# The weighted selection matrix of layer 1, made on GpSimd in thirds, one pair ahead

## The chip, the core and the metric

The kernel runs on one core of a Trainium2 chip. A core has TensorE (matrix products, PE in the profile), VectorE (DVE), ScalarE (ACT), GpSimd (POOL) and SyncE (SP), which here only issues transfers. Each engine executes its own list of instructions in order, and semaphores make an engine wait for another one or for a transfer. The metric is device time in microseconds.

## The reference, cut to what matters

There are 128 graphs of 64 nodes with 128 features, and one weighted adjacency matrix per graph. About a quarter of its entries are not zero. Four layers follow one another, each with a residual and a layer norm. Layers 0 and 1 compute a filter for every edge and sum messages over a node's edges. Layers 2 and 3 are graph convolutions. Layer 1, which the change is about, is in short:

```python
diff = e[:, :, :, None] - offsets              # 64 gaussians of each edge weight
g = jnp.exp(coeff * diff * diff)
h = ssp(einsum('bijg,fg->bijf', g, W1) + b1)   # ssp is softplus - log 2
Wf = einsum('bijf,gf->bijg', h, W2) + b2       # the filter of edge i, j
rf = einsum('bjd,fd->bjf', r, Wa)
Wf = Wf * Am                                   # Am is the edge weight
y = einsum('bjf,bijf->bif', rf, Wf * Am)       # so each message has the weight squared
y = einsum('bid,ed->bie', ssp(einsum('bif,df->bid', y, Wd1) + bd1), Wd2) + bd2
x = layernorm(x + y)
```

## The kernel before, in words

The first stage packs the edges. Rows are sorted by their number of edges, and each pair of graphs gets lists of "slots", one slot for each edge that is kept, with three values: d (the edge weight), j (the number of the source node, as bf16) and w (the factor of the message; in layer 1 the weight squared). The lists lie in DRAM, written by `pack`.

The main loop takes one pair of graphs after the other, number n from 0 to 127. Pairs 0 to 63 are layer 0, pairs 64 to 127 are layer 1 (`NP` is 64 and `N` is 128). Partitions 0 to 63 belong to the first graph of a pair, 64 to 127 to the second. A pair is worked on in three steps, k = 0, 1, 2, each on a third of its slots; in layer 1 a third has 380 to 420 columns (`CHUNKS`). The loop is a software pipeline over steps i = 3n + k:

- `loads(n + 2)`, at k = 0, issues on SP the transfers of d, j and w for the pair two ahead, in the order d, j, w for each of the two graphs (line 1289). d has three buffers in rotation, j and w two.
- `gaussians(n + 1, k)` makes the gaussians in place in d on ScalarE, for the next pair (a `Square` at k = 0, an `Exp` at k = 1).
- `one_hot(n)`, at k = 0, makes the weighted selection matrix `hot` on VectorE (line 1750). Its row r, column s is w of slot s where j of slot s equals r, and 0 elsewhere. It has two buffers in rotation.
- `filter_in` multiplies the gaussians by W1 (`px`, line 1762), and ScalarE makes the softplus `h`.
- `gather`, for the step before, multiplies the node features by a third of `hot` (`pg`, line 1789): this selects and weighs the source node of each slot. ScalarE copies it to `g`.
- `filter_out` and `message`, for the step before that, multiply `h` by W2 (`pw`, line 1776) and, on VectorE, multiply by `g` (`m`, line 1804). `slot_sums` adds each row's slots (lines 1828 and 1832).

Pairs are joined in groups of four for the work on nodes. `node_after` makes layer 1's output for a group and its layer norm, then `graph_convs` does layers 2 and 3 for it. These are generators: `slot(queue)` runs one piece of one of them at a set place in each step, so that the pieces lie between the pieces of the edges. `layernorm` takes statistics on VectorE (`mv`, line 1401). For groups of four pairs the rest is GpSimd's: `rs` (lines 1407 and 1408) and four scalings (line 1413). A group has three such norms: `x_all<-ny` after layer 1, `x_all<-gz` after layer 2 and `gz<-gz` after layer 3. TensorE's transposes `gx` (line 1673) read the first, its product `sup` (line 1662) the second. After the third the output is stored, one pair a step, by an indirect transfer from GpSimd (`out_dram<-gz`, line 1029). GpSimd also adds constant rows to `x_all` (lines 1434 and 1677) and fills `blocks` (`scaled`, line 1616).

The order on every engine in the loop is the order in which the program writes the instructions: `in_order` chains all instructions of an engine, SP's and GpSimd's too. So an instruction that waits holds back everything behind it on its engine.

Each piece of the edge work goes with a position like

```python
if n > 0:
    one_hot(n)
```

and the change touches one such position and adds another.

Of the kernel before, what the change touches and what calls it, by code (L numbers as in the profile page):

```python
# [12 lines left out]
F32 = mybir.dt.float32  # L13
AF = mybir.ActivationFunctionType
ALU = mybir.AluOpType
# [4 lines left out]
P = 128  # L20
# [46 lines left out]
CHUNKS = tuple(tuple(n // 3 for n in sizes) for sizes in GSLOTS)  # L67
MAX_SLOTS, MAX_CHUNK = max(map(max, GSLOTS)), max(map(max, CHUNKS))
# [533 lines left out]
def sparse_stack(ctx: ExitStack, tc: tile.TileContext, t: dict, out: bass.AP, flag):  # L602
# [11 lines left out]
    nc = tc.nc  # L614
    x, adj = t["x"], t["adj"]
    NB = x.shape[0]
    NP = NB // 2
# [10 lines left out]
    edge = ctx.enter_context(tc.tile_pool(name="sedge", bufs=2))  # L628
    ps_n = ctx.enter_context(tc.tile_pool(name="sps_n", bufs=2, space=PSUM))

    def pair_at(n):

        return n // NP, (n + 8 * (n // NP)) % NP
# [57 lines left out]
    near = row[:, 3:4]  # L691
# [78 lines left out]
    for b in range(2):  # L770
        for k in range(3):
            at = slice(A * b + NG0 * k, A * b + NG0 * (k + 1))
            nc.scalar.dma_start(fw1[at, k, :], t["L0_gnn_fw1"])
        at = slice(A * b, A * b + 3 * NG0)
# [15 lines left out]
    def run(queue, n):  # L790

        held = None
        while queue and n:
            try:
                held = next(queue[0])
                n -= 1
            except StopIteration:
                queue.popleft()
        return held
# [139 lines left out]
    def act(out_, in_, func, **kw):  # L939
        nonlocal fence, latest, kind  # L940
        now = func == AF.Sin
        if kind is None or now != kind:
            fence = latest
            if not now:
                ctx_ = tc.issue_after(fence.ins) if fence is not None else nullcontext()
                with ctx_:
                    fence = nc.scalar.preload_act_table_set("natural_log_exp_and_others")
            kind = now
        with tc.issue_after(fence.ins) if fence is not None else nullcontext():
            latest = nc.scalar.activation(out_, in_, func, **kw)  # L950
        return latest
# [323 lines left out]
    def loads(n, engine=nc.sync):  # L1275


        layer, p = pair_at(n)
        s = p // 8
        size = GSLOTS[layer][s]  # L1280
        at = (p % 8) * 2 * size
        assert (layer, s) in stored, "slots are read before they are written"
        d = edge.tile([P, MAX_SLOTS], F32, tag="d", name=f"d_{n}", bufs=3)
        j = edge.tile([P, MAX_SLOTS], BF16, tag="j", name=f"j_{n}")
        w = edge.tile([P, MAX_SLOTS], F32, tag="w", name=f"w_{n}")

        def load(to, name, first, n):

            (engine if name == "d" else nc.sync).dma_start(to, dram_ap(slots[layer, name][s], first, [[0, to.shape[0]], [1, n]]))  # L1289

        third = size // 3
        d = d[:, 0 : size if layer else third]
        for b in range(2):
            rows, first = slice(A * b, A * (b + 1)), at + b * size
            if layer == 1:
                load(d[rows], "d", first, size)
            else:
                for k, end in enumerate((NG0, 2 * NG0, A)):
                    load(d[A * b + NG0 * k : A * b + end], "d", first + k * third, third)
            load(j[rows, 0:size], "j", first, size)  # L1300
            load(w[rows, 0:size], "w", first, size)
        return d, j, w
# [18 lines left out]
    permuted_rows, goes, hots = {}, {}, {}  # L1321
# [54 lines left out]
    def by_pair(v):  # L1376
        return v.rearrange("p (s c) -> p s c", c=P)
# [146 lines left out]
    def load_nodes(layer, q):  # L1524

        first, n = GROUPS[layer][q].start, GROUPS[layer][q].stop - GROUPS[layer][q].start
        codes = node.tile([P, GS * P], BF16, tag="cb", name=f"cb_{layer}_{q}")[:, 0 : n * P]
        nc.sync.dma_start(codes, dram_ap(code_dram[layer], first * P, [[0, P], [1, n * P]]))
        node_codes[layer, q] = codes
        if layer == 0:  # L1530
            rows = node.tile([P, GS, A], F32, tag="zr", name=f"zr_{q}")
            for s in range(GS):
                nc.sync.dma_start(rows[:, s, :], perm[first + s][:, 0:A])
            zero_rows[q] = rows
# [106 lines left out]
    def normals_of(q):  # L1641

        for i in (2, 3):
            scaled(i, q)
            yield
            at = GROUPS[1][q].start - GS
            nT = small[i][:, at : at + blocks[q].shape[1], :]
            yield from normal(i, q, nT)
            yield
            normals[i, q] = nT  # L1650
# [86 lines left out]
    def gaussians(n, step):  # L1737
        d, w = slot_data[n][0], layers[n // NP]
        if step == 0:
            act(d, d, AF.Square, scale=-1.0, bias=w["off"])  # L1740
        else:
            act(d, d, AF.Exp, scale=w["coeff"])

    def one_hot(n):

        _, j, wt = slot_data[n]
        layer, p = pair_at(n)
        size = GSLOTS[layer][p // 8]
        hots[n] = edge.tile([P, MAX_SLOTS], F32, tag="hot", name=f"hot_{n}")
        nc.vector.scalar_tensor_tensor(  # L1750
            hots[n][:, 0:size], j[:, 0:size], near, wt[:, 0:size], ALU.is_equal, ALU.mult
        )

    def filter_in(c):

# [13 lines left out]
    def softplus(c):  # L1769
        act(c["h"], c["h"], AF.Ln, scale=0.5, bias=half)  # L1770
# [95 lines left out]
    N = 2 * NP  # L1866
# [8 lines left out]
    gaussians(0, 0)  # L1875
    gaussians(0, 1)
    one_hot(0)
    early = deque([gathering()])

    def ahead(n):  # L1880

        layer, p = pair_at(n + GS)
        for q, group in enumerate(GROUPS[layer]):
            if group.start == p:
                befores.append(node_before(layer, q))
# [3 lines left out]
    def slot(queue):  # L1889


        nonlocal owing
        before, owing = owing, None
        held = run(queue, 1)
        if before is not None and before is not queue:
            run(before, 1)
        if held:
            owing = queue
# [8 lines left out]
    for i in range(3 * N + 2):  # L1907
        n, k = divmod(i, 3)
        c, c1, c2 = None, *past


        run(sums, (1, 4, 4)[k])
        run(early, 9 if i < 18 else (PACE - 2, PACE + 1, PACE + 1)[k] if i < 3 * (NP - 8) else 7)
        run(side, min(2, len(side)))
        run(stores, 1)
        if i == 3 * (NP + 5):
            assert not early and not side and not convs[0], "edges are still to be gathered"
            compacting.close()
            rings.append(ctx.enter_context(tc.tile_pool(name="srings", bufs=4)))
            for q in (0, 1, *small_groups):  # L1920
                group = GROUPS[1][q]
                blocks[q] = rings[0].tile(
                    [P, group.stop - group.start, P], F32, name=f"blocks{q}", bufs=1
                )
                nc.gpsimd.memset(blocks[q], 0.0)

            small[2] = by_pair(node.tile([P, GS * P], F32, tag="zt", name="small2", bufs=1))
            small[3] = zblk
        if n < N:
            layer, p = pair_at(n)  # L1930
            q = next(q for q, group in enumerate(GROUPS[layer]) if group.start <= p < group.stop)
            c = dict(
                id=f"{n}_{k}", n=n, k=k, s=p - GROUPS[layer][q].start, at=(layer, q), w=layers[layer],
                size=CHUNKS[layer][p // 8],
            )
            if k == 0:
                if n + GS < N:
                    ahead(n)
                if n + 2 < N:
                    slot_data[n + 2] = loads(n + 2)  # L1940
                if c["s"] == min(2, len(range(NP)[GROUPS[layer][q]]) - 1):
                    load_nodes(layer, q)
                if n > 0:
                    one_hot(n)
                if layer == 1 and c["s"] == 0 and q in last:
                    last[q].append(normals_of(q))
            filter_in(c)
        if c1 is not None:
            gather(c1)
        if c is not None:  # L1950
            softplus(c)
            if k == 2 and sines:

                sines.popleft()()
        slot(nodes)
        if k == 1 and befores:
            slot(befores)
        for queue in last.values():
            slot(queue)
        if c2 is not None:  # L1960
            filter_out(c2)
            message(c2)
        if convs[0]:
            slot(convs[0])
        if k < 2 and n + 1 < N:
            gaussians(n + 1, k)
        slot(convs[1])
        for queue in last.values():
            slot(queue)
        past = [c, c1]  # L1970
# [53 lines left out]
```

## Time and profile before

| | |
|---|---|
| median of 3 runs | 1656.86 us (1652.58 to 1659.53) |
| profiled execution | 1684.44 us |
| its span, first to last instruction | 1682.6 us |
| mean granted TensorE clock | 0.961 |
| PE busy | 1474.7 us (88%) |
| DVE busy | 1481.3 us (88%) |
| ACT busy | 1279.8 us (76%) |
| POOL busy | 738.2 us (44%) |
| `hot` on DVE, 128 instructions | 179.0 us |
| layer 1's share of the span, about | 795 to 1683 us |

The profile comes from one execution, taken by the hardware profiler. "Busy" is the time in which an engine executes instructions; issuing transfers and waiting on semaphores don't count. A group of instructions is written as line, engine, operation, output<-inputs. The idle time in front of an instruction is put down to the event that ended it, its releaser. The chain of waits goes back from an instruction to what released it, and so on. The matmuls' ends are modelled, so a busy TensorE need not be at its peak. Spans on GpSimd are rough.

### The profile page before, as it was taken

The numbers are of one execution on the slowest core, as the hardware profiler recorded it, in microseconds if no ns is written. First come the engines' busy times: TensorE is split into PE (matmuls) and PEld (weight loads), VectorE is DVE, ScalarE is ACT, GpSimd is POOL, SyncE is SP. The second block draws the span as 40 slices with busy tenths as digits, with TensorE's granted clock in tenths as the row PEclk, the third lists the DMA queues.
The fourth block names the chain that finished last, engine by engine and source line by source line (L and its number), as shares of the span: only waits on it lengthen the run. The fifth ranks groups of instructions, "written<-read, shape, count | busy, mean of one in ns | idle before, by whom it ended". The sixth has DMA issues, their size and how long they took to land.

```text
span 1682.6 us, 24560 instructions
## 1 busy us (share of the span) xinstructions
PE 1474.7 (88%) x6813; PEld 816.6 (49%) x6813; DVE 1481.3 (88%) x4032; ACT 1279.8 (76%) x1723; POOL 738.2 (44%) x1180
## 2 busy tenths in 40 slices
PE   0177898999989989998999999999999999998976
PEld 0133454444545545555445555555555555554544
DVE  6677999999998999999888989999999989898874
ACT  1166797878878878887999878888888888787742
POOL 2325155454554533443422355445455335454444
PEclk9999999999999999998999999999999999999975
DMA  7644364545545454444665555555555544466100
GB/s 243 187 113 112 93 142 119 136 121 134 129 108 123 112 136 111 117 114 116 154 154 134 132 118 134 140 121 127 135 122 126 133 119 111 112 141 138 43 8 22
DMA packets 122294, 205.70 MB, mean 122 GB/s; under 512 B 47957, under 2 KB 80035, under 8 KB 121507
## 3 DMA queue, kind: packets, MB, share of 16 engines
q1 hardware_dynamic: 110784, 187.61, 46.1%
q0 software_dynamic: 6576, 14.99, 2.7%
q10 hardware_dynamic: 4786, 1.43, 0.4%
q8 instruction: 57, 0.93, 0.2%
q14 instruction: 91, 0.74, 0.2%
HBM read 185.29 MB, written 18.64 MB: 121 GB/s over the span
## 4 chain that ended last, share of the span: by engine, by line
DVE 32%; PE 25%; DMA 12%; ACT 11%; POOL 9%; issue 7%; SPq 3%; another core or an unknown queue 0%; ACTq 0%; DVEq 0%; POOLq 0%
DVE m L1804 9%; PE pw L1776 9%; DMA out_dram<-gz,at_row 6%; PE px L1762 6%; ACT h L950 5%; DVE agg L1828 5%; PE pg L1789 4%; DVE hot L1750 4%; POOL gz L1413 2%; POOL x_all L1413 2%; SPq L1289 2%; DVE at L1178 2%; ACT g L950 2%; ACT d L950 2%; POOL rs L1408 2%
## 5 line engine op out<-in xcount | busy, mean ns | idle before, releaser
L950 ACT ACTIVATE g<-pg 128x672 f32<-128x672 f32 (+12 forms) x384 | 302.4, 788 | 69.1 <-DVE m L1804 53.8
L950 ACT ACTIVATE h<-h,half 128x672 f32<-128x672 f32 (+13 forms) x385 | 351.4, 913 | 0.1
L1828 DVE TENSOR_REDUCE agg<-m 128x16 f32<-128x240 f32 (+13 forms) x896 | 326.0, 413 | 2.4
L1789 PE MATMUL pg<-hot,ys 64*128 64x336 f32 (+12 forms) x1536 | 316.9, 489 | 10.1 <-DVE hot L1750 7.5
L1776 PE MATMUL pw<-h,w_L_gnn_W2T 128*128 128x420 f32 (+5 forms) x768 | 305.8, 521 | 1.5 <-DVE m L1804 1.5
L1776 PE MATMUL pw<-h,w_L_gnn_fw 128*128 128x336 f32 (+6 forms) x768 | 267.9, 472 | 37.5 <-DVE m L1804 31.8
L950 ACT ACTIVATE h<-px,c_L_gnn_b 128x840 f32<-128x840 f32 (+5 forms) x192 | 178.2, 928 | 120.0 <-PE px L1762 117.2
L1804 DVE SCALAR_TENSOR_TENSOR m<-pw,c_L_gnn_b,g 128x420 f32<-128x420 f32 (+5 forms) x384 | 227.2, 628 | 26.3 <-PE pw L1776 18.4
L1804 DVE SCALAR_TENSOR_TENSOR m<-pw,c_L_gnn_fb,g 128x336 f32<-128x336 f32 (+6 forms) x384 | 202.0, 568 | 26.8 <-PE pw L1776 10.2
L1762 PE MATMUL px<-d,fw 64*128 64x336 f32 (+6 forms) x768 | 169.5, 518 | 54.1 <-DMA d<-d_dram 32.0
L950 ACT ACTIVATE h<-px,c_L_gnn_fb 128x672 f32<-128x672 f32 (+6 forms) x192 | 158.5, 825 | 67.1 <-PE px L1762 50.5
L1789 PEld LDWEIGHTS pg<-hot,ys 64*128 64x128 f32 x1536 | 149.4, 192 | 117.0 <-issue 25.0
L1776 PEld LDWEIGHTS pw<-h,w_L_gnn_fw 128*128 128x128 f32 x768 | 134.3, 194 | 132.4 <-DVE m L1804 74.0
L1776 PEld LDWEIGHTS pw<-h,w_L_gnn_W2T 128*128 128x128 f32 x768 | 134.2, 193 | 130.2 <-issue 30.8
L1750 DVE SCALAR_TENSOR_TENSOR hot<-j,row,w 128x1212 f32<-128x1212 bf16 (+12 forms) x128 | 179.0, 1398 | 9.1 <-DMA w<-w_dram 9.1
L1762 PE MATMUL px<-d,w1t 64*128 64x420 f32 (+5 forms) x768 | 184.1, 557 | 0.1
L1407 POOL TENSOR_SCALAR rs<-mv 128x4 f32<-128x4 f32 x61 | 23.8, 390 | 271.3 <-DVE mv L1401 269.6
L950 ACT ACTIVATE d<-d,neg_off 128x1212 f32<-128x1212 f32 (+12 forms) x128 | 119.4, 933 | 26.0 <-DMA d<-d_dram 13.1
L1762 PEld LDWEIGHTS px<-d,fw 64*128 64x128 f32 x768 | 60.4, 191 | 147.0 <-issue 55.0
L1029 POOL DMA_INDIRECT rows<-comb,goes x64 | 71.4, 1115 | 99.9 <-DMA rows<-comb,goes 71.0
L1413 POOL TENSOR_SCALAR x_all<-ny,mv,rs 128x128 f32<-128x128 f32 x124 | 104.0, 847 | 3.3
L1029 POOL DMA_INDIRECT out_dram<-gz,at_row x56 | 70.4, 1256 | 53.2 <-DMA out_dram<-gz,at_row 40.6
(267 smaller groups left out, 2240.9 us busy)
## 6 DMA issues: line engine op xcount, KB each, us to landing
d<-d_dram SPq DMA_DIRECT2D x32, 315.0 KB
w<-w_dram SPq DMA_DIRECT2D x32, 315.0 KB
d<-d_dram SPq DMA_DIRECT2D x32, 303.0 KB
w<-w_dram SPq DMA_DIRECT2D x32, 303.0 KB
w<-w_dram SPq DMA_DIRECT2D x32, 252.0 KB
j<-j_dram SPq DMA_DIRECT2D x32, 157.5 KB
j<-j_dram SPq DMA_DIRECT2D x32, 151.5 KB
d<-d_dram SPq DMA_DIRECT2D x16, 300.0 KB
```

What stands on the lines that cost most here:

```text
L950: latest = nc.scalar.activation(out_, in_, func, **kw)
L1029: nc.gpsimd.indirect_dma_start(out=into, out_offset=bass.IndirectOffsetOnAxis(ap=at, axis=0), in_=rows, in_offset=None,)
L1178: nc.vector.max_index(out=at[:, r, cut], in_max=top[:, r, cut], in_values=av[:, r, :])
L1289: (engine if name == "d" else nc.sync).dma_start(to, dram_ap(slots[layer, name][s], first, [[0, to.shape[0]], [1, n]]))
L1408: nc.gpsimd.tensor_tensor(rstd, rstd, neg_half[:, 0:n], ALU.pow)
L1413: (nc.gpsimd if n == GS else nc.vector).tensor_scalar(dst[:, s, :], y[:, s, :], mv[:, s, 0:1], rstd[:, s : s + 1], ALU.subtract, ALU.mult,)
L1750: nc.vector.scalar_tensor_tensor(hots[n][:, 0:size], j[:, 0:size], near, wt[:, 0:size], ALU.is_equal, ALU.mult)
L1762: nc.tensor.matmul(ps[:, b, 0:n], lhsT=w1, rhs=d[rows, col : col + n], start=True, stop=True)
L1776: nc.tensor.matmul(ps[:, 0 : c["size"]], lhsT=c["w"]["w2"], rhs=c["h"][:, b, :], start=True, stop=True)
L1789: nc.tensor.matmul(ps[:, b, 0:n], lhsT=y[rows, :], rhs=hots[c["n"]][rows, at], start=True, stop=True,)
L1804: nc.vector.scalar_tensor_tensor(messages[n][:, b, at], c["pw"][b][:, 0:size], c["w"]["b2"], c["g"][:, b, :], ALU.add, ALU.mult,)
L1828: nc.vector.tensor_reduce(av[:, :, :, r], both, AX.X, ALU.add)
```

## The change

For pairs 0 to 64 nothing changes: `one_hot(n)` makes the whole matrix on VectorE at k = 0 of the pair itself. For pairs 65 to 127 it is made on GpSimd, in the three steps of the pair before, a third in each. A third takes two instructions: a comparison of j with the partition's row number, written as 1.0 or 0.0 into `hot`, and a product in place with w. The call stands behind `gaussians` and in front of `slot(convs[1])` in the step.

```diff
-    def one_hot(n):
+    def one_hot(n, third=None):
 
         _, j, wt = slot_data[n]
         layer, p = pair_at(n)
         size = GSLOTS[layer][p // 8]
-        hots[n] = edge.tile([P, MAX_SLOTS], F32, tag="hot", name=f"hot_{n}")
-        nc.vector.scalar_tensor_tensor(
-            hots[n][:, 0:size], j[:, 0:size], near, wt[:, 0:size], ALU.is_equal, ALU.mult
-        )
+        if third in (None, 0):
+            hots[n] = edge.tile([P, MAX_SLOTS], F32, tag="hot", name=f"hot_{n}")
+        if third is None:
+            nc.vector.scalar_tensor_tensor(
+                hots[n][:, 0:size], j[:, 0:size], near, wt[:, 0:size], ALU.is_equal, ALU.mult
+            )
+        else:
+            k = CHUNKS[layer][p // 8]
+            at = slice(third * k, (third + 1) * k)
+            nc.gpsimd.tensor_scalar(hots[n][:, at], j[:, at], near, None, ALU.is_equal)
+            nc.gpsimd.tensor_tensor(hots[n][:, at], hots[n][:, at], wt[:, at], ALU.mult)
...
-                if n > 0:
+                if 0 < n <= NP:
                     one_hot(n)
...
         if k < 2 and n + 1 < N:
             gaussians(n + 1, k)
+        if NP <= n < N - 1:
+            one_hot(n + 1, k)
         slot(convs[1])
```

## The prediction

> **What bounds the kernel now.** I read the page first: engine totals, slices, costliest groups. The columns of a group are busy time, mean ns of one, idle time before it and its releaser.
>
> ```profile
> DVE  6677999999998999999888989999999989898874
> POOL 2325155454554533443422355445455335454444
> ...
> L1750 DVE SCALAR_TENSOR_TENSOR hot<-j,row,w 128x1212 f32<-128x1212 bf16 (+12 forms) x128 | 179.0, 1398 | 9.1 <-DMA w<-w_dram 9.1
> ...
> L1413 POOL TENSOR_SCALAR x_all<-ny,mv,rs 128x128 f32<-128x128 f32 x124 | 104.0, 847 | 3.3
> ```
>
> VectorE is nearly full and GpSimd looks half empty. That is an average. Second, therefore, the chain of waits in one stretch of layer 1 (start us, us, what):
>
> ```profile
> 1220.82 3.15 POOL gz L1413 x4
> ...
> 1224.14 4.26 DMA out_dram<-gz,at_row
> ...
> 1229.16 4.41 DMA out_dram<-gz,at_row
> ...
> 1237.71 3.15 POOL x_all L1413 x4
> ...
> 1240.91 0.33 PE gx L1673
> ```
>
> Here the chain goes through GpSimd for 21 us: normalise, store, wait for the store's landing, store, wait again, normalise, and TensorE starts `gx` only then. Third, GpSimd's own timeline (start, us, instruction, idle time before it in brackets):
>
> ```profile
> 1229.16 0.96 POOL L1029 DMA_INDIRECT out_dram<-gz,at_row  x1 [3.34 <-DMA out_dram<-gz,at_row]
> 1233.70 0.61 POOL L1616 TENSOR_TENSOR blocks<-a_all,dinv 64x256 f32<-64x256 f32 x1 [2.93 <-DMA out_dram<-gz,at_row]
> 1249.74 3.14 POOL L1413 TENSOR_SCALAR x_all<-gz,mv,rs 128x128 f32<-128x128 f32 x4
> 1269.12 0.23 POOL L1407 TENSOR_SCALAR rs<-mv 128x4 f32<-128x4 f32 x1 [16.25 <-DVE mv L1401]
> ```
>
> The same list repeats with every group of four pairs. It has three parts. Part one runs from the third norm's `rs` (1219.36) to the end of `x_all<-ny` (1240.86): 21.5 us, 6.3 us of it waiting for stores. Part two runs to the end of `x_all<-gz` (1252.88): 12.0 us, 1.2 of it waiting. Part three is the gap to the next `rs` at 1269.12, 16.3 us, in which GpSimd waits. Sum 49.8 us. Twelve such groups start between 964.92 and 1531.85; in the later ones the gap is up to 19.8 us.
>
> Fourth, the waits between 840 and 1610 us (in total, times, longest):
>
> ```profile
> PEld gx L1673 <- POOL x_all L1413: 21.5, 32, 1.6
> PEld pw L1776 <- DVE m L1804: 16.6, 29, 1.4
> PE gx L1673 <- POOL x_all L1413: 12.5, 27, 1.0
> ```
>
> TensorE already waits for GpSimd in `gx`, and `sup` starts within 0.5 us of the end of `x_all<-gz` in the groups at 1199 and 1249 (some 2 us after it in later ones). TensorE is 197 of 200 us busy from 1000 to 1200 and executes in order, so GpSimd's parts one and two have next to no slack, and only the gap has room.
>
> **What the Trainium skill says.** GPSIMD Engine Reference, § 3.1, gives about 2.6 cycles an element for a two-input product. The trace agrees: `x_all` plus a row (L1434) takes 456 ns at 128 wide and 1278 at 512, so 2.14 ns an element. The same page, § 4.1, calls one-input operations roughly line rate. This trace doesn't agree for scalar operations: L1413 takes 785 ns for 128 elements. SBUF — State Buffer, § Who interferes with whom: a VectorE instruction with two SBUF inputs excludes a GpSimd one that reads SBUF. The removed operation is of that kind, so its removal gives GpSimd a little back; `x_all` groups of 3.9 to 4.3 us instead of 3.14 may be that, though the trace names no cause.
>
> **The change, part by part.**
>
> *Removed*: 63 selection matrices on VectorE (pairs 65 to 127) at about 1.4 us, 88 us busy. The chain shows what they are worth: `hot` is 2.0% of 860 to 1000, 4.2% of 1000 to 1200, at most four pieces in 1200 to 1400, 2.7% of 1400 to 1600, so 2.8 + 8.4 + at most 6 + 5.4, some 22 us at most. Nearly all of it lies in the gap, where VectorE leads to the next `mv`.
>
> *Added*: 189 thirds on GpSimd, each a comparison and a product over 380 to 420 columns, say 400. The product, from L1434: 456 + 272 x 2.14 = 1038 ns. The comparison (bf16 in, f32 out, one scalar per partition) has no row. Below: a converting copy (L1201), 446 ns for 320, about 0.52 us for 400. Above: L1413 with two scalars, 0.785 us at 128 against 0.235 at 4 wide (L1407), 4.4 ns an element, 2.0 us. Nearest: one-operation `dc` (L1095), 238 ns at 10 and 297 at 31 wide, 2.8 ns an element, 1.33 us; I take this. The product waits for its comparison, 0.1 us as between L1407 and L1408. A third is 2.5 us (1.65 to 3.1); all 189 are 470 us (310 to 590) on an engine that has about 95 of each 200 us filled.
>
> *Where the thirds stand*: GpSimd's order of the changed program repeats with two groups. Part one gets three or four thirds, part two two or three, the gap six.
>
> Part one, with three: norm 4.6, third 2.5, so the first store starts at 7.3 instead of 4.8 and lands 4.3 us later, 11.6; the next third ends at 11.5, inside that wait; the second store starts at 12.3; the second half of `blocks` waits for its landing, 16.7, and ends at 17.4; third, 19.9; third store, 21.1; norm and `x_all`, 26.1. With four it is 26.0, one more being inside a wait. Before 21.5: 4.5 more. The store waits hide the rest; without that cover it would be 7.5 to 10.
>
> Part two: 12.0 less the wait of 1.2, plus 2.5 thirds on average (6.25) is 17.05: 5.0 more, less 1 us of slack before `sup`: 4.0 more.
>
> Gap: six thirds are 15.0 us in 16.3 or more: hidden. The chain without `hot` could be 1.5 us shorter, but 15.0 plus waits is the floor: 0.5 less.
>
> Sum: 4.5 + 4.0 - 0.5 = 8.0 us a group, times 12 = 96 us. Before 965 us there are few norms and no stores, and TensorE sets the pace: nothing, or a few us either way. Layer 0 and the tail after 1610 us keep their work.
>
> *Moved*: a pair's j and w must have landed a whole pair earlier. Around 1224 VectorE finishes `hot` at 1224.84, SP issues j, w, d, j, w to 1227.9 and traffic falls off at 1233.1. The first third of that pair is called for at about 1235. It waits itself in GpSimd's queue, and its buffer comes free earlier than now by up to a step of 3.9 us. So I price it at nothing, covered by some 2 to 6 us; if uncovered, d for the second graph stands behind j and w on SP, `Square` on ScalarE waits, and it costs perhaps 2 us a pair. A ready matrix has four steps until its matmul, so `pg` itself won't wait for long. Two matrices in rotation, as before: the new wait on TensorE's previous read is over by then.
>
> The profiled execution is 1684.44 us (span 1682.6, the rest lies around it), 1.7% above the median 1656.86. 1684 + 96 = 1780 profiled, 5.7% more; for the median I take 1657 + 95 = **1752 us**.
>
> **Rivals.**
> - *Cheap comparison*: 0.52 us, a third 1.65. Part one +3.1, part two +1.9, gap -1.3: 3.7 a group, 44 us, 1701 us. For it: casts run so. Against: every TENSOR_SCALAR here is dearer. Chance 0.18.
> - *GpSimd full throughout*: a third of 3.1 us. Part one +5.9, part two +5.5, gap 18.6 us against 16.3 to 19.8, +0.9: 12.3 a group, 148 us, 1805 us. For it: the rate of L1413. Chance 0.17.
> - *Loads late*: j and w, with d behind them, hold `Square`; 2 us in each of the 48 pairs of the twelve groups over the forecast, 1848 us at worst, about half of it likely. Against: the margin above. Chance 0.06.
> - *Faster*: VectorE is the bound (the first row is all 8s and 9s), the gap shortens by what `hot` has of the chain and the thirds stay out of the way: 22 us less, 1635 us. It decides only where a third costs less than about 0.9 us: at that size about four thirds a group, 3.6 us, equal the waits, slack and chain they can fill. The product alone is 1.04, so `x_all` would need slack that the view of waits doesn't show. Chance 0.04.
>
> **How the numbers follow.** The forecast has 0.55. Its own range, a third from 2.1 to 2.8 us and a group from 5.7 to 10, is 1722 to 1780. Adding the cheap and the full case gives 1690 to 1815. A measurement of this kernel tells some 0.5%, 8 us, from no change. Faster 0.04; within it 0.02, the far end of the cheap case, with more slack than I can see; slower 0.94.
>
> **What would show it.** The comparison near 1.3 us and the product near 1.05; GpSimd over 80% busy from 965 to 1590; groups of 57 to 59 us; waits for stores in part one cut from 6.3 to about 3.5 us; `gx` and `sup` waiting for `x_all` 4 us each a group; TensorE at 85% there; `hot` gone from VectorE's chain in layer 1. Wrong: a third under 1.7 us, gaps that stay at 16 us in front of `rs`, or `pg` or `Square` with the largest new wait.

## The result and the profile after

The changed kernel takes 1749.31 us (median, 1743.72 to 1751.25) where the kernel before, beside it, takes 1658.19: a ratio of 1.0566, 95% interval [1.0529, 1.0602], 91 us slower. Its profiled execution took 1751.25 us with a span of 1749.4.

On the page, the two rows that the prediction began with, and the two groups that are new (busy us and mean ns, then idle time and its releaser):

```profile
DVE  7599999999989999896788688677775876776774
POOL 2424464545646334349878888888898888988844
...
L1758 POOL TENSOR_SCALAR hot<-j,row 128x404 f32<-128x404 bf16 (+5 forms) x189 | 249.3, 1319 | 34.1 <-PE pg L1796 28.8
...
L1759 POOL TENSOR_TENSOR hot<-hot,w 128x404 f32<-128x404 f32 (+5 forms) x189 | 197.5, 1045 | 15.8
```

From the slice in which layer 1 begins, the rows have changed places: GpSimd reads mostly 8s and 9s where it read 4s, and VectorE mostly 6s to 8s where it read 8s and 9s. The new work is 447 us of GpSimd in place of 96 of VectorE, whose matrices took 179.0 us and now take 82.9.

The chain of waits in one group of layer 1 (start us, us, what), whose third norm starts at 1248.68:

```profile
1253.24 1.28 POOL hot L1758
...
1254.60 1.02 POOL hot L1759
...
1259.75 3.72 DMA out_dram<-gz,at_row
...
1264.31 1.28 POOL hot L1758
...
1270.24 2.33 POOL x_all L1413 x3
...
1277.52 1.25 POOL hot L1758
...
1283.91 3.13 POOL x_all L1413 x4
...
1287.08 0.49 PE sup L1662 x2
```

In the stretch shown of before, the chain went through GpSimd only up to `gx`. Now it stays on GpSimd from the third norm to `sup`, with the thirds as its links, and between them the norms that TensorE waits for.

GpSimd's own timeline in the next group, at the bounds of the three parts (start us, us, instruction, idle time before it in brackets):

```profile
1302.59 0.23 POOL L1407 TENSOR_SCALAR rs<-mv 128x4 f32<-128x4 f32 x1 [1.08 <-DVE mv L1401]
...
1317.48 1.06 POOL L1029 DMA_INDIRECT out_dram<-gz,at_row  x1 [1.43 <-DMA out_dram<-gz,at_row]
...
1325.10 3.12 POOL L1413 TENSOR_SCALAR x_all<-ny,mv,rs 128x128 f32<-128x128 f32 x4
...
1342.64 3.12 POOL L1413 TENSOR_SCALAR x_all<-gz,mv,rs 128x128 f32<-128x128 f32 x4
...
1357.14 1.24 POOL L1758 TENSOR_SCALAR hot<-j,row 128x384 f32<-128x384 bf16 x1 [4.45 <-PE pg L1796]
...
1364.50 0.23 POOL L1407 TENSOR_SCALAR rs<-mv 128x4 f32<-128x4 f32 x1
```

Part one lasts from 1302.59 to 1328.22, 25.6 us; part two to 1345.76, 17.5; the gap to 1364.50, 18.7. The group before it, with one third fewer in each of the first two parts, has 23.9, 14.5 and 15.6 us. So groups alternate between some 54 and 61 us. The group of before that the prediction dissected has 21.5, 12.0 and 16.3, but it is the shortest of its kernel: over eleven groups, from the first third norm in this stretch on, the means are 22.3, 11.3 and 17.9 us before and 25.0, 16.2 and 17.2 now.

The waits between 840 and 1680 us (in total, times, longest):

```profile
ACT h L950 <- PE px L1769: 188.2, 105, 8.5
PEld gx L1673 <- POOL x_all L1413: 51.6, 44, 4.5
POOL hot L1758 <- PE pg L1796: 28.8, 10, 5.0
PEld sup L1662 <- POOL x_all L1413: 25.9, 32, 2.8
POOL blocks L1616 <- DMA out_dram<-gz,at_row: 19.7, 14, 2.6
POOL rs L1407 <- DVE mv L1401: 16.9, 10, 2.6
```

and of before, in the same part of the program, which ends earlier there (840 to 1610 us):

```profile
POOL rs L1407 <- DVE mv L1401: 258.9, 16, 30.6
ACT h L950 <- PE px L1762: 116.2, 90, 5.7
```

`gx` waited 21.5 us there, `sup` 0.6. GpSimd waited 258.9 us for VectorE's `mv`, now 16.9: its idle time is used up. ScalarE's softplus, behind TensorE's waits, went from 116.2 to 188.2.

**Where the time is.** From the start of VectorE's last matrix (pair 64's) to the last `pg`, layer 1 takes 897.9 us where it took 812.7, 85.2 more. Over eleven intervals between third norms the mean went from 51.5 to 58.4 us, which is 75.3 of it; 7.9 fall before the first of these groups and 2.0 after the last. What follows the last `pg` is as long as before. The medians differ by 91; the profiled execution of before had spent some 19 us more in layer 0 with the same instructions, so whole spans aren't compared here.

One part of this is in no term of the prediction. Over layer 1 (795.5 to 1609 us before, 776 to 1674.5 now) TensorE does the same matmuls (3661 and 3659 in the traces) but is busy 825.7 us with them instead of 788.2, at a granted clock of 0.95 instead of 0.98; its idle time grows from 25 to 73 us. So 37 of the 85 us show up as slower matmuls and 48 as idle time. Whether the slower matmuls lengthen the groups, or only fill time in which TensorE would have waited for GpSimd, no run separates.

### The profile page after: what moved, and what is told of

The parts are those of the page before. It is cut to its first block, busy times and chain, and to the rows that moved or that the text cites. A ratio compares the mean times of both kernels' runs of the same rounds, so it can differ in the third digit from the quotient of the medians.

```text
span 1749.4 us, 25003 instructions
## 1 busy us (share of the span) xinstructions
PE 1508.0 (86%) x6813; PEld 827.8 (47%) x6813; DVE 1409.0 (81%) x3969; ACT 1281.0 (73%) x1723; POOL 1156.5 (66%) x1558
## 3 DMA queue, kind: packets, MB, share of 16 engines
q10 hardware_dynamic: 4786, 1.43, 0.4%
## 4 chain that ended last, share of the span: by engine, by line
PE 30%; POOL 23%; DVE 19%; DMA 11%; issue 6%; SPq 5%; ACT 5%; ACTq 0%; POOLq 0%; DVEq 0%
PE pw L1783 10%; PE px L1769 6%; POOL hot L1758 6%; DVE m L1811 5%; PE pg L1796 5%; POOL hot L1759 4%; POOL x_all L1413 4%; DMA out_dram<-gz,at_row 4%; SPq L1289 3%; DVE agg L1835 3%; DVE hot L1752 2%; ACT h L950 2%; POOL rs L1408 2%; DMA w<-w_dram 2%; DMA d<-d_dram 2%
## 5 line engine op out<-in xcount | busy, mean ns | idle before, releaser
L1796 PE MATMUL pg<-hot,ys 64*128 64x336 f32 (+12 forms) x1536 | 325.2, 501 | 13.8 <-DVE hot L1752 7.5
L1783 PE MATMUL pw<-h,w_L_gnn_W2T 128*128 128x420 f32 (+5 forms) x768 | 310.3, 528 | 1.2 <-DVE m L1811 1.2
L1811 DVE SCALAR_TENSOR_TENSOR m<-pw,c_L_gnn_b,g 128x420 f32<-128x420 f32 (+5 forms) x384 | 231.7, 629 | 92.6 <-PE pw L1783 81.3
L1758 POOL TENSOR_SCALAR hot<-j,row 128x404 f32<-128x404 bf16 (+5 forms) x189 | 249.3, 1319 | 34.1 <-PE pg L1796 28.8
L1811 DVE SCALAR_TENSOR_TENSOR m<-pw,c_L_gnn_fb,g 128x336 f32<-128x336 f32 (+6 forms) x384 | 201.4, 564 | 17.9 <-PE pw L1783 8.3
L1759 POOL TENSOR_TENSOR hot<-hot,w 128x404 f32<-128x404 f32 (+5 forms) x189 | 197.5, 1045 | 15.8
L1769 PE MATMUL px<-d,w1t 64*128 64x420 f32 (+5 forms) x768 | 191.6, 577 | 1.6 <-ACT h L950 1.6
L1769 PEld LDWEIGHTS px<-d,w1t 64*128 64x128 f32 x768 | 60.3, 192 | 67.0 <-ACT h L950 26.7
```

The lines of the kernel that those rows point to most:

```text
L1758: nc.gpsimd.tensor_scalar(hots[n][:, at], j[:, at], near, None, ALU.is_equal)
L1759: nc.gpsimd.tensor_tensor(hots[n][:, at], hots[n][:, at], wt[:, at], ALU.mult)
L1769: nc.tensor.matmul(ps[:, b, 0:n], lhsT=w1, rhs=d[rows, col : col + n], start=True, stop=True)
L1783: nc.tensor.matmul(ps[:, 0 : c["size"]], lhsT=c["w"]["w2"], rhs=c["h"][:, b, :], start=True, stop=True)
L1796: nc.tensor.matmul(ps[:, b, 0:n], lhsT=y[rows, :], rhs=hots[c["n"]][rows, at], start=True, stop=True,)
L1811: nc.vector.scalar_tensor_tensor(messages[n][:, b, at], c["pw"][b][:, 0:size], c["w"]["b2"], c["g"][:, b, :], ALU.add, ALU.mult,)
```

## The experiments

My theory was that of the prediction: a third costs its time where it stands in front of a norm of its group, and little in the gap. The rivals were that the matrix or its loads come too late, that VectorE was the bound, and that GpSimd's total load decides wherever the load stands. Times beside the kernel before, which had medians of 1654 to 1657 us in these comparisons.

### Idle thirds beside VectorE's matrices

GpSimd gets two instructions of about a third's size (380 or 384 columns) on other data, whose result nobody reads. VectorE keeps its matrices and no load moves:

```diff
+    other = a_all.rearrange("p n j -> p (n j)")
+    into = fw1.rearrange("p k c -> p (k c)")
+    def idle(n):
+        layer, p = pair_at(n)
+        k = CHUNKS[layer][p // 8]
+        k = min(k, 3 * C)
+        nc.gpsimd.tensor_scalar(into[:, 0:k], other[:, 0:k], near, None, ALU.is_equal)
+        nc.gpsimd.tensor_tensor(into[:, 0:k], into[:, 0:k], other[:, 0:k], ALU.mult)
...
             gaussians(n + 1, k)
+        if NP <= n < N - 1 and True:
+            idle(n + 1)
```

> The kernel before, with the whole matrix still made on VectorE; at the places of the thirds GpSimd makes a comparison and a product of 384 columns that nobody reads. Theory (GpSimd's time in front of x_all is what costs): the change's +91 us, plus what VectorE no longer saves, at most 22: 1749 to 1775 us. Rival A (the cost lies in the matrix or its loads coming at another time): near 1658, at most 1675.

Two further kernels do this for half of the pairs alone: those whose thirds stand in parts one and two (`(n + 1) % GS in (0, 1)` in place of `True`), and those whose thirds stand in the gap (`in (2, 3)`; in every second group one of the six stands behind the third norm instead).

> As the run above, with the idle thirds only for the first and second pair of each group of four, which are the thirds that lie in parts one and two. Theory: these are the ones that cost, +65 to +100 us: 1723 to 1758. Rival B (GpSimd's sum of work counts wherever it lies): half of the full run's cost, some +50: 1708. Rival A: near 1658.

> The idle thirds only for the third and fourth pair of each group, which are the thirds that lie in the gap. Theory: 14 us fit into a gap of 16 to 20, -2 to +15 us: 1656 to 1673. Rival B: some +50: 1708. Rival A: near 1658.

Measured: all thirds 1796.08 us, ratio 1.0863 [1.0811, 1.0915], 142 more; those of parts one and two 1767.81, 1.0677 [1.0626, 1.0727], 114 more; those of the gap 1683.9, 1.0177 [1.0130, 1.0224], 30 more. The halves add up to the whole (144 and 142). The same instructions cost almost four times as much in front of the norms as in the gap, so load alone doesn't decide. And thirds of which nobody needs the result cost more than the change itself, so it needs no late matrix or load to be slower. All three are above what I had expected.

Waits of the kernel with thirds in parts one and two, 840 to 1680 us:

```profile
POOL rs L1407 <- DVE mv L1401: 213.5, 15, 18.9
PEld gx L1673 <- POOL x_all L1413: 64.0, 44, 5.1
```

and of the one with thirds in the gap:

```profile
POOL rs L1407 <- DVE mv L1401: 105.5, 17, 18.3
PEld gx L1673 <- POOL x_all L1413: 34.9, 43, 2.0
```

The first keeps 213.5 us of GpSimd idle in front of `mv` and is the slow one: its TensorE waits 64.0 us for `gx`. The second fills the gap and loses little at `gx`.

From GpSimd's timelines, the mean lengths of the three parts over eleven groups (us; one profiled execution of each kernel; the last two kernels follow below). The execution of before is 27.6 us over that kernel's median and some 19 of them lie in layer 0, so its groups may be up to some 0.7 us too long, by this estimate:

| | part one | part two | gap | sum |
|---|---|---|---|---|
| before | 22.3 | 11.3 | 17.9 | 51.5 |
| the change | 25.0 | 16.2 | 17.2 | 58.4 |
| all idle thirds | 26.8 | 17.3 | 18.0 | 62.0 |
| idle thirds in parts one and two | 26.3 | 17.1 | 17.1 | 60.5 |
| idle thirds in the gap | 23.2 | 10.6 | 19.5 | 53.4 |
| no matrices | 19.4 | 10.8 | 18.6 | 48.9 |
| all idle thirds, no matrices | 25.3 | 16.8 | 17.0 | 59.1 |

Thirds in parts one and two lengthen just these two. Of the kernel with thirds in the gap, part one is 23.9 us in the six groups that have a third there and 22.4 in the five others, so about 9 of its 30 us, by this estimate, are not the gap's.

### No matrices in layer 1

```diff
-                if n > 0:
+                if 0 < n <= NP:
                     one_hot(n)
+                elif n > NP:
+                    hots[n] = hots[NP]
```

> The kernel before without the matrices of pairs 65 to 127, on either engine: these pairs gather with the matrix of pair 64, so the output is not the reference's. It prices what VectorE is relieved of. Theory: at most the 22 us that the chain shows, 1636 to 1655. Rival C (VectorE is the bound of layer 1): most of the 88 us, 1570 to 1600.

Measured: 1631.3 us, ratio 0.9865 [0.9819, 0.9911], 23 us less, a little below the range that I had named. That is what VectorE's 96 us of matrices are worth where no one else makes them. Part one is 2.9 us shorter and the gap isn't shorter at all (the table above). VectorE isn't the bound, and the rival that took it for the bound falls.

### Idle thirds and no matrices

The idle thirds cost 142 us, the absence of the matrices gains 23; the change, which does both, should then lose 119 and loses 91. Something of some 28 us was missing from the account. In the kernel with all idle thirds, GpSimd's instructions were longer; one example from its timeline, both engines (start us, us, engine, instruction):

```profile
1302.07 1.53 DVE L1750 SCALAR_TENSOR_TENSOR hot<-j,row,w 128x1176 f32<-128x1176 bf16 x1
1302.44 2.30 POOL L1677 TENSOR_TENSOR x_all<-x_all,b_L_gnn_b 128x512 f32<-128x512 f32 x1
```

The GpSimd instruction takes 2.30 us where it takes 1.28 on its own. It starts 0.37 us after VectorE's matrix began and ends 1.14 us after that ended, about as if it had been stopped until then. So both edits together:

> Before, with the idle thirds of the first experiment on GpSimd (two instructions whose result nobody reads) and, beside them, without VectorE's matrices in layer 1 (pair 64's stands in for all, so it leaves out the weighting of the other pairs). Idle thirds alone cost 142 us and the matrices' absence alone gains 23. If the two only add up, 1765 to 1785 us. If VectorE's matrices also stretch GpSimd's instructions while both run, taking them away gives back more with the thirds than without: 1740 to 1755 us, as after. The comparison's mean then falls from 1413 to about 1320 ns.

Measured: 1748.84 us, ratio 1.0550 [1.0496, 1.0605]: the same as the change (1.0566). With the thirds there, the matrices' absence is worth 47 us by the medians and 52 by the ratios, without them 23. The groups of GpSimd's instructions from 965 to 1590 us, with matrices on VectorE:

```profile
L1762 POOL TENSOR_SCALAR fw<-a_all,row 128x384 f32<-128x384 f32 (+1 forms) x122 | 171.8, 1408 | 7.4
...
L1616 POOL TENSOR_TENSOR blocks<-a_all,dinv 64x256 f32<-64x256 f32 x40 | 31.1, 778 | 8.6 <-DMA out_dram<-gz,at_row 7.7
L1677 POOL TENSOR_TENSOR x_all<-x_all,b_L_gnn_b 128x512 f32<-128x512 f32 x10 | 17.2, 1716 | 0.4
```

and without:

```profile
L1762 POOL TENSOR_SCALAR fw<-a_all,row 128x384 f32<-128x384 f32 (+1 forms) x127 | 159.9, 1259 | 7.7
...
L1616 POOL TENSOR_TENSOR blocks<-a_all,dinv 64x256 f32<-64x256 f32 x43 | 26.3, 613 | 38.6 <-DMA out_dram<-gz,at_row 38.1
L1677 POOL TENSOR_TENSOR x_all<-x_all,b_L_gnn_b 128x512 f32<-128x512 f32 x11 | 14.1, 1280 | 0.4
```

The comparison falls from 1408 to 1259 ns, `blocks` from 778 to 613, the added row from 1716 to 1280, though none of them was edited. The Trainium skill (SBUF — State Buffer, § Who interferes with whom) says that a VectorE instruction with two SBUF inputs contends with a GpSimd instruction that reads SBUF; these runs agree, and give the size: up to 1 us for one that is met, 0.15 us in the mean for a comparison. That exclusion is the cause is the page's statement; the runs show the stretch and that it goes with the matrices.

This kernel has neither the earlier loads of j and w nor the new wait for TensorE's read, and takes the same time as the change, with thirds that are some 0.08 us shorter (1259 and 1001 ns against 1315 and 1029 in the same stretch). By the rate of the next experiment the shorter thirds alone should make it 6 us faster than the change; by the ratios it is 3 us faster, with an interval of some 11 us either way. So the loads and the wait together cost the change nothing that these runs can tell, at most some 8 us, and not its 91.

### A third of half the length

The change without its product:

```diff
             nc.gpsimd.tensor_scalar(hots[n][:, at], j[:, at], near, None, ALU.is_equal)
-            nc.gpsimd.tensor_tensor(hots[n][:, at], hots[n][:, at], wt[:, at], ALU.mult)
```

> After the change, with the product left out: GpSimd only compares, so the matrix lacks its weights and what is computed is not the reference. The order, the waits and the loads of j and w stay; a third falls from about 2.4 us (1.29 + 1.04 + a wait) to about 1.35. If the time of the thirds in GpSimd's order is the cause, the prediction's own sums (96 us at 2.5 us a third, 44 at 1.65) go on to about 26 us at 1.35: 1670 to 1700 us. If the early call for j and w, or the two matrices in rotation, set the time, it stays above 1735.

Measured: 1671.09 us, ratio 1.0072 [1.0044, 1.0099], about 12 more than before. At 2.4 us a third the loss is 91, at 1.35 some 12 to 14, and without any matrix there is a gain of 23. So the last 1.05 us of a third cost 73 to 75 us per microsecond, and the first 1.35 us only 26 to 27 (12 to 14 and the 23, divided by 1.35). That is what the room in front of the norms looks like from outside: a little is free, then nearly everything counts. The steps aren't quite clean, for in this kernel GpSimd also waits 70.9 us for TensorE's reads and 12.5 for the landing of j, and what these cost no run shows.

### The wait for TensorE's read of the matrix

The two matrices become one tile, so that a third waits only for TensorE's read of the same third two pairs before:

```diff
+    hot_two = edge.tile([P, 2, MAX_SLOTS], F32, tag="hot", name="hot_two", bufs=1)
...
-            hots[n] = edge.tile([P, MAX_SLOTS], F32, tag="hot", name=f"hot_{n}")
+            hots[n] = hot_two[:, n % 2, :]
```

> After the change, with the two matrices in one tile, so that the first comparison of a pair waits only for TensorE's read of the same third two pairs before, not of the whole matrix. The trace of after shows 28.8 us of such waits in GpSimd, of up to 10 us, most of them in every second group and in its gap, where the group is some 7 us longer. If a wait in the gap delays the next norm, most of it comes back: 1718 to 1738 us. If GpSimd would only have waited for VectorE's mv instead, it stays at 1744 to 1754.

Measured: 1741.95 us, ratio 1.0491 [1.0460, 1.0522], 7 us under the change by the medians and 12 by the ratios; neither of the two ranges that I had named. (The expectation gives the waits as up to 10 us; it is ten waits of up to 5.0.) The waits of this kernel, 840 to 1680 us:

```profile
POOL rs L1407 <- DVE mv L1401: 37.5, 15, 7.2
...
POOL hot_two L1760 <- PE pg L1798: 1.0, 2, 0.6
```

The wait of 28.8 us is gone, and 20.6 of it have become a wait for `mv` (16.9 in the change, 37.5 here). In the gap GpSimd would have waited anyway for most of that time. In the profiles layer 1 is only 3 us shorter than in the change (894.9 us against 897.9), so 7 and 12 are on the high side; their intervals reach some 8 us either way.

### Only the pairs of the gap on GpSimd

From the change, VectorE keeps the matrices of the other pairs:

```diff
+    def on_gpsimd(n):
+        return n % GS in (2, 3)
...
-                if 0 < n <= NP:
+                if 0 < n <= NP or n > NP and not on_gpsimd(n):
                     one_hot(n)
...
-        if NP <= n < N - 1:
+        if NP <= n < N - 1 and on_gpsimd(n + 1):
             one_hot(n + 1, k)
```

> After the change, but only every second two pairs (those whose thirds GpSimd makes in its gap between two groups of norms) get their matrix from GpSimd; the others stay on VectorE as before. Idle thirds in the gap alone cost 30 us; half of VectorE's relief is worth some 12 us, and some exclusion goes with it. If place decides, 1655 to 1680 us, at best equal to before. If the count of thirds decides, half of after's loss, about 1700 us. If VectorE's relief is worth more than the thirds in the gap, below 1650 us, better than both kernels.

Measured: 1659.56 us, ratio 1.0015 [0.9996, 1.0033]: no difference from before that can be told. Half of the thirds stay on GpSimd, and all of the loss is gone. With `return n % GS == 2`, one pair of four:

> After the change, but only one pair of every four gets its matrix from GpSimd: the one whose three thirds stand right behind the norm of the second graph (x_all<-gz), first in the gap. The other three stay on VectorE. 16 matrices leave VectorE: a quarter of the 23 us that all are worth, some 6 us. Their thirds, 7 us, stand in a gap of 16 to 20. If thirds with room in the gap cost nothing, 1647 to 1655 us with the kernel before at 1656, a ratio of about 0.997. If even they delay something, as 30 us for six thirds a gap would say of three taken pro rata, some 15 less 6 us: 1662 to 1670, a ratio of about 1.006.

Measured: 1651.96 us, ratio 0.9976 [0.9956, 0.9996]: some 4 us faster than before, between 1 and 7. Its waits, 840 to 1680 us:

```profile
POOL rs L1407 <- DVE mv L1401: 165.7, 18, 23.3
...
PEld gx L1673 <- POOL x_all L1413: 12.5, 25, 0.9
```

GpSimd still waits 165.7 us for `mv`, and `gx` waits no longer than before (12.5 us against 21.5). The gain is small, and less than the 8 us that the prediction had called the least a measurement tells, but many runs of both kernels went into it (22 and 27), and its sign is that of thirds with room. Of the kernels that leave nothing out it is the fastest.

The pairs of the gap with the two matrices in one tile:

> The kernel with two pairs of every four on GpSimd, and the two matrices in one tile so that its first comparison waits only for TensorE's read of the same third two pairs before. In the profile of that kernel GpSimd waits 26 us for TensorE's reads, up to 4.7 us, in the gap in front of the next norm. If these set the time of the next norm, some 5 to 12 us come back: 1648 to 1655 us, under the kernel before. If VectorE's mv or the landing of j and w then ends the gap instead, it stays within 3 us of 1659.

Measured: 1675.11 us, ratio 1.0111 [1.0078, 1.0145], 15 us slower than without that edit. The edit seems to have had a second effect, on the rotation of j's buffers: one pair in four then gets the buffer of a pair that GpSimd reads last, where it had been that of one that VectorE reads. The traces don't name buffers, so this is read from the waits: SP's loads wait 63.2 us for VectorE's matrices, where they waited 129.7, and longer for GpSimd's. SP's waits, 965 to 1590 us, with one tile:

```profile
SPq L1289 <- POOL hot_two L1760: 199.8, 20, 16.3
```

and with two:

```profile
SPq L1289 <- POOL hot L1758: 61.3, 17, 5.9
```

SP stands up to 16.3 us in front of that load with the later pairs' d, j and w behind it, and GpSimd waits 23.1 us, in four waits of up to 6.0, for the landing of j. So this run says nothing of the wait it was made for, which stays untested in this kernel. Its 15 us are probably what late loads cost, but nothing parts the two.

## Why the prediction was right, and where it wasn't

**The verdict and its cause** stand: 1752 us forecast, 1749.31 measured, because thirds stand in front of `gx` and `sup` on GpSimd. The idle thirds in two places show it directly. The forecast for the profiled execution, 1780 us, was 29 too high, since it began from the one of before, which had lost some 19 us in layer 0.

**The third** was priced at 2.5 us. The comparison's median is 1.29 us (1.33 forecast), the product's 1.04 (1.04), the wait between them 0.07 to 0.09: 2.4. Rates from neighbouring rows, the one-operation `dc` and the added row, were good to 3%. The "roughly line-rate" that the Trainium skill (GPSIMD Engine Reference, § 4.1) gives for operations with one input isn't borne out here: GpSimd's comparison alone takes 1.27 us for 392 columns, while VectorE made the whole matrix, 1176 columns with both operations, in about 1.44.

**Part one**, +4.5: from 22.3 to 25.0 us in the mean of eleven groups, so +2.7. The price of the thirds was right: idle ones beside VectorE's matrices make it 4.5 longer. What was misplaced is the relief from the matrices, "nearly all of it" in the gap by the prediction: without them part one is 2.9 us shorter, and the gap isn't. The sum also let the second store and `blocks` wait 3.5 us for landings; in the two groups of the result they wait 2.14 and 1.43. Mis-sized by 1.8 us a group, on the dear side.

**Part two**, +4.0: from 11.3 to 16.2, so +4.8. The 1 us of slack that the forecast took off is mostly not there.

**Gap**, −0.5: from 17.9 to 17.2, so −0.7. The size is right, the reasons only in part. "The new wait on TensorE's previous read is over by then" was wrong: it is 28.8 us in ten waits, up to 5.0. It was worth some 3 to 12 us, not 28.8, since `mv` wasn't ready much sooner. And "hidden" is a little too good for thirds without relief: five or six idle ones lengthen the gap by 1.6 us. Three of them with one matrix less on VectorE cost nothing.

**Sum**: 2.7 + 4.8 − 0.7 is 6.9 us a group before rounding, against 8.0 forecast. Part two, too cheap, makes up for some of part one, too dear; and the 7.9 us in front of the first group, "nothing, or a few us either way", make up for more. That the number is closer than its terms is luck.

**Not priced**: the exclusion of VectorE's matrices, which I had given "a little". With thirds on GpSimd it is worth some 24 to 29 us (47 to 52, less 23), a credit to the change. It was in none of the terms. Beside idle thirds the matrices' absence shortens part one by 1.5 us, part two by 0.5 and the gap by 1.0; how much of each is exclusion and how much VectorE's relief, no run separates. Nor was a slower TensorE priced, with its 37 us of longer matmuls.

**VectorE's relief**, at most 22 us: 23 measured, though for 96 us of matrices, not 88 (1.52 us each, not 1.4), and in another place. **Moved loads**, at nothing: right, within the 8 us that the runs can tell. In the trace of the changed kernel SP stands up to 14.0 us in front of these loads (965 to 1590 us), and still no wait of GpSimd's thirds or of `Square` ends with a landing of d, j or w (840 to 1680 us).

**What would show it**: GpSimd is 86 to 88% busy and groups are 58.4 us long, as said. `gx` waits 51.6 us, about 4 a group; `sup` 25.9, only 2. TensorE wasn't at 85%. Windows of 200 us, the first line of before and the other two of the changed kernel, read (busy us and instructions of PE, PEld, DVE, ACT, POOL, then the granted clock):

```profile
1000.00:1200.00 200.00, 197.03 (x940) 111.11 (x938) 188.16 (x424) 171.63 (x208) 96.68 (x109) 1.00 0.55 130
...
1000.00:1200.00 200.00, 188.56 (x849) 104.24 (x849) 152.12 (x367) 154.16 (x185) 173.64 (x177) 0.95 0.48 115
1200.00:1400.00 200.00, 180.24 (x790) 98.61 (x790) 141.84 (x347) 141.99 (x173) 171.56 (x180) 0.92 0.43 106
```

From 1000 to 1200 us TensorE does 849 matmuls where it did 940, 10% fewer, and is busy 188.56 us where it was 197.03. A matmul takes 222 ns in the mean, 210 before, at a granted clock of 0.95 instead of 1.00. Here the share of busy time doesn't fall in step with the work, since the clock falls too.

**Rivals**: the cheap comparison and the full GpSimd fell with the third's size, late loads and a faster kernel with the runs above. The latter's point of decision, 0.9 us a third, fits what was measured: a straight line between nothing (23 us less) and 1.35 us (12 to 14 more) crosses zero at 0.84 to 0.89, and the curve, which bends upward, at that or somewhat later.

## What to carry to other kernels

An engine that is 47% busy, as GpSimd was in layer 1, may have no room where it matters: cut its time at the instructions that others wait for, and place new work only in the stretch that ends in a wait for someone else. Here a quarter of the moved work, put there, was worth a small gain, half of it, mostly there, was worth nothing, and all of it cost 91 us. Make idle copies of the new work, in one place at a time, before moving anything: they price the place without the rest of the change.

## What the hardware showed that I had not expected

A GpSimd instruction that reads SBUF while VectorE runs a matrix with two SBUF inputs took up to 1 us longer here (2.30 us instead of 1.28), VectorE's own mean staying at 1.52 us as before. So the costs of two engines don't simply add up: removing 63 such VectorE instructions was worth 23 us with GpSimd half idle and 47 to 52 us with it 87% busy.
